# Strassen's partial sums kept in PSUM banks, adj and transition turned through DRAM and VectorE, layer norms applied on ScalarE, fewer weight loads and a longer lag, in a two-layer graph network kernel

## The chip, the cores and the metric

One core of one Trainium2 chip. The metric is the device time of one launch in microseconds (us), the median of several runs. A ratio of two kernels is the mean time of one kernel's fast runs over that of the other's fast runs of the same rounds on the same chip, so it is not quite the ratio of the medians quoted beside it.

## The reference

128 graphs of 128 nodes with 512 features; everything is fp32. Cut to what matters:

```python
# layer 0
deg = sum(adj, -1);  agg = (adj @ x) / max(deg, 1e-6)
y   = layernorm(x + relu(concat([x, agg]) @ W.T))
# layer 1: attention scores make a transition matrix, then K = 3 diffusion steps
e   = leaky_relu(sj[:, None] + si[:, None].T + ab)       # sj, si: y @ Wv @ aw
T   = adj * exp(e);  T = T / (sum(T, -1) + 1e-12)
H   = y @ Wk[0] + bk[0]  +  (T @ y) @ Wk[1] + bk[1]  +  (T @ T @ y) @ Wk[2] + bk[2]
out = layernorm(y + relu(H))
```

Both layers have the form "a product with weights, then a product with a 128x128 matrix of the graph".

## The kernel before

Two graphs make a pair, four a group; 64 pairs in all. The pair's products with weights are done in Strassen's way, with seven products of half the depth instead of eight, on sums of blocks. A product is two wide fp32 matmuls. The seven have to be combined: in the kernel before, ScalarE copies snapshots of a growing PSUM sum to SBUF, and VectorE adds them off to the side:

```python
def fused_pair(name, lf, rf, mT):              # used for layer 0 ("h") and the diffusion ("v")
    X, Y, W, V = ...                           # four PSUM banks; s: four SBUF snapshots
    product(X, 1, lf, rf, True);   nc.scalar.copy(s[0], X)
    product(Y, 2, lf, rf, True);   nc.vector.tensor_add(u[:, 0], Y, s[0])
    product(W, 5, lf, rf, True);   nc.scalar.copy(s[1], W)
    product(X, 6, lf, rf, False);  nc.scalar.copy(s[2], X)
    product(V, 4, lf, rf, True)
    product(X, 7, lf, rf, False);  nc.scalar.copy(s[3], X)
    nc.vector.tensor_add(u[:, 1], V, s[3])
    product(W, 3, lf, rf, False)
    nc.tensor.matmul(W, mT[0], u[:, 0], start=False, ...)   # product with adj or transition
    nc.tensor.matmul(X, mT[1], u[:, 1], start=False, ...)
    return (W, s[2]), (X, s[1])                # the caller adds the last snapshot

def layernorm(t):                              # VectorE, GpSimd, VectorE
    nc.vector.bn_stats(st, t);  nc.vector.bn_aggr(mv, st)
    nc.gpsimd.tensor_scalar(ve, mv[:, 1:2], LN_EPS, None, ALU.add)
    nc.gpsimd.tensor_tensor(rstd, ve, nhalf, ALU.pow)
    nc.vector.tensor_scalar(t, t, mv[:, 0:1], rstd, ALU.subtract, ALU.mult)
```

One step of the main loop runs layer 0 of a pair and layer 1 of the pair two steps earlier, so TensorE has two independent streams. The order of each engine's own instructions is set by a scheduler at build time. The traces show it kept: a sum whose inputs are there waits behind what was queued before it (the prediction below shows an add that ran 4.4 us late in this way). After layer 0's product, each of the two graphs gets its layer norm and two score sums (`scr`, VectorE, with a running sum as by-product).

Of the kernel before, what the change touches and what calls it, by code (L numbers as in the profile page):

```python
# [15 lines left out]
def kernel(  # L16
# [29 lines left out]

    nc = tc.nc
    P = 128
# [10 lines left out]
    const = ctx.enter_context(tc.tile_pool(name="const", bufs=1))  # L59
    p2 = ctx.enter_context(tc.tile_pool(name="p2", bufs=2))  # L60
    p1 = ctx.enter_context(tc.tile_pool(name="p1", bufs=1))
    p3 = ctx.enter_context(tc.tile_pool(name="p3", bufs=3))
    p4 = ctx.enter_context(tc.tile_pool(name="p4", bufs=4))
    dram = ctx.enter_context(tc.tile_pool(name="dram", bufs=3, space=bass.MemoryType.DRAM))
    small = ctx.enter_context(tc.tile_pool(name="small", bufs=4))
    ps_t = ctx.enter_context(tc.tile_pool(name="ps_t", bufs=2, space=bass.MemoryType.PSUM))
    ps_m = ctx.enter_context(tc.tile_pool(name="ps_m", bufs=6, space=bass.MemoryType.PSUM))
# [6 lines left out]
    def load_blocks(dst, src):  # L74

        for q in range(Q):
            nc.sync.dma_start(dst[q * R : (q + 1) * R].rearrange("r b j f -> r (b j) f"),
                              src[:, :, q * P : (q + 1) * P].rearrange("b (j r) f -> r (b j) f", r=R))
# [14 lines left out]


    def load_weight(dst, src):

        for q in range(Q):
            nc.sync.dma_start(dst[q * R : (q + 1) * R],
                              src[q * P : (q + 1) * P, :].rearrange("(c s) o -> s c o", s=R))

    load_x_blocks(0, 0)
    load_adj(0, nc.scalar)
    w0_sb = const.tile([P, 2 * NC, F], FP)
    wk_sb = const.tile([P, K, NC, F], FP)
    wvt_sb = [p4.tile([P, H, F], FP, name=f"wvt{i}", tag="y") for i in range(2)]
# [4 lines left out]
    load_weight(w0_sb[:, NC:, :], w0t[F:, :])  # L110
    load_weight(w0_sb[:, :NC, :], w0t[:F, :])
    load_x_blocks(0, 1)
    load_x(0, 0)
# [3 lines left out]
    nc.scalar.dma_start(bk_sb, bk)  # L117
    for i in range(2):
        nc.scalar.dma_start(wvt_sb[i], wvt[i * FH : (i + 1) * FH, :].rearrange("(c p) f -> p c f", p=P))
    load_adj(1, nc.scalar)  # L120
    load_x_blocks(1, 0)
    for k in range(K - 1, -1, -1):
        load_weight(wk_sb[:, k], wk[k])
# [5 lines left out]
    onesk = const.tile([K, P], FP)  # L129
    nc.gpsimd.memset(onesk, 1.0)  # L130
# [11 lines left out]
    w2, w1 = w0_sb[:, NC:, :], w0_sb[:, :NC, :]  # L142
# [8 lines left out]
    def fold_constants():  # L151
        for t in range(2):
            pw = ps_m.tile([P, F], FP, name="pw", tag="mm")
            for c in range(NC):
                nc.tensor.matmul(pw, aw_sb[:, t, c : c + 1].to_broadcast([P, P]), wvt_sb[c // H][:, c % H, :],
                                 start=(c == 0), stop=(c == NC - 1))
            nc.scalar.copy(wrow[:, t, :], pw)
        pb = ps_m.tile([P, F], FP, name="pb", tag="mm")
        nc.tensor.matmul(pb, onesk, bk_sb, start=True, stop=True)  # L159
        nc.scalar.copy(bias, pb)  # L160
        pc = ps_m.tile([P, F], FP, name="pc", tag="mm")
        for t in range(2):
            for c in range(NC):
                nc.tensor.matmul(pc[:, :1], bv_sb[:, c : c + 1].to_broadcast([P, P]), aw_sb[:, t, c : c + 1],
                                 start=(t == 0 and c == 0), stop=(t == 1 and c == NC - 1))
        nc.vector.tensor_add(cc, pc[:, :1], ab_sb)


    def transposed(dst, src):

        p = ps_t.tile([P, 4, P], FP, name="pt", tag="tr")
        for c in range(4):
            nc.tensor.transpose(p[:, c, :], src[:, c, :], ident)  # L173
        nc.scalar.copy(dst, p)

    def left_factors(pool, name, src):

        t = pool.tile([P, 7, H, P], FP, name=name)
        a11, a12, a21, a22, s1, s2, s4 = (t[:, i] for i in range(7))
        for i in range(2):  # L180
            nc.vector.transpose(t[:, 2 * i : 2 * i + 2].rearrange("p a h (j r) -> p j (a h) r", r=R),  # L181
                                src[:, i].rearrange("p j (c s) -> p j c s", s=R))
        nc.vector.tensor_add(s1, a21, a22)
        nc.vector.tensor_sub(a21, a11, a21)
        nc.gpsimd.tensor_sub(s2, s1, a11)
        nc.gpsimd.tensor_sub(s4, a12, s2)
        return [None, a11, a12, s4, a22, s1, s2, a21]

    def product(dst, i, lf, rf, start, stop=True):
        for c in range(H):  # L190
            nc.tensor.matmul(dst, lf[i][:, c, :], rf[i][:, c, :], start=(start and c == 0),  # L191
                             stop=(stop and c == H - 1), skip_group_check=True)

    def fused_pair(name, lf, rf, mT):


        X, Y, W, V = (ps_m.tile([P, F], FP, name=f"{name}{n}", tag="mm") for n in "xywv")
        s = [pool.tile([P, F], FP, name=f"snap{j}") for j, pool in enumerate((p1, p2, p2, p1))]
        u = p2.tile([P, 2, F], FP, name="u")
        product(X, 1, lf, rf, True)  # L200
        nc.scalar.copy(s[0], X)
        product(Y, 2, lf, rf, True)
        nc.vector.tensor_add(u[:, 0], Y, s[0])
        product(W, 5, lf, rf, True)
        nc.scalar.copy(s[1], W)
        product(X, 6, lf, rf, False)
        nc.scalar.copy(s[2], X)
        product(V, 4, lf, rf, True)
        product(X, 7, lf, rf, False)
        nc.scalar.copy(s[3], X)  # L210
        nc.vector.tensor_add(u[:, 1], V, s[3])  # L211
        product(W, 3, lf, rf, False)
        nc.tensor.matmul(W, mT[0], u[:, 0], start=False, stop=True, skip_group_check=True)  # L213
        nc.tensor.matmul(X, mT[1], u[:, 1], start=False, stop=True, skip_group_check=True)  # L214
        return (W, s[2]), (X, s[1])

    def layernorm(t):
        st = small.tile([P, 6], FP, name="st")
        nc.vector.bn_stats(st, t)  # L219
        mv = small.tile([P, 2], FP, name="mv")  # L220
        nc.vector.bn_aggr(mv, st)  # L221
        ve = small.tile([P, 1], FP, name="ve")
        nc.gpsimd.tensor_scalar(ve, mv[:, 1:2], LN_EPS, None, ALU.add)  # L223
        rstd = small.tile([P, 1], FP, name="rstd")
        nc.gpsimd.tensor_tensor(rstd, ve, nhalf, ALU.pow)  # L225
        nc.vector.tensor_scalar(t, t, mv[:, 0:1], rstd, ALU.subtract, ALU.mult)  # L226

    xfs, aTs, ys, ybs, yfs, scs, Ts, TTs = {}, {}, {}, {}, {}, {}, {}, {}
# [4 lines left out]
    def degree_norm(g):  # L233
# [6 lines left out]
        nc.vector.tensor_mul(an, adjs[g], rdeg[:, :, None].to_broadcast([P, G, N]))  # L240
        aTs[g] = p2.tile([P, G, N], FP, name="aT")
        transposed(aTs[g], an)

    def layer0(g, p):

        ys[g, p] = p4.tile([P, 2, F], FP, name="y")
# [5 lines left out]
        for i, (ph, s) in enumerate(hs):  # L252
            b = 2 * p + i
            y = ys[g, p][:, i, :]
            nc.vector.tensor_add(y, ph, s)
            nc.vector.scalar_tensor_tensor(y, y, 0.0, xs[g, p][:, i, :], ALU.max, ALU.add)
# [15 lines left out]
    def transition(g):  # L272
# [7 lines left out]
        T = p2.tile([P, G, N], FP, name="T")  # L280
# [10 lines left out]
        Ts[g] = T  # L291

    def t_transpose(g):
        TTs[g] = p2.tile([P, G, N], FP, name="TT")
        transposed(TTs[g], Ts[g])

    def layer1(g, p):
# [3 lines left out]
        v1 = p2.tile([P, 2, F], FP, name="v1", tag="u")  # L301
        for i, (pv, s) in enumerate(fused_pair("v", lf, f1, tT)):
            nc.vector.tensor_add(v1[:, i], pv, s)

        Q0, Q1 = (ps_m.tile([P, F], FP, name=f"o{i}", tag="mm") for i in range(2))
        Y, W, V, X = Q0[:, :FH], Q0[:, FH:], Q1[:, :FH], Q1[:, FH:]
        s = p1.tile([P, 2, F], FP, name="so")
        product(X, 1, lf, f2, True)
        nc.scalar.copy(s[:, 0, :FH], X)
        product(Y, 2, lf, f2, True)  # L310
        product(W, 5, lf, f2, False)
        nc.scalar.copy(s[:, 1, FH:], W)
        product(X, 6, lf, f2, False)
        nc.scalar.copy(s[:, 0, FH:], X)  # L314
        product(W, 3, lf, f2, False)
        product(X, 7, lf, f2, False)
        nc.scalar.copy(s[:, 1, :FH], X)  # L317
        nc.tensor.matmul(Q0, tT[0], v1[:, 0], start=False, stop=True, skip_group_check=True)  # L318
        product(V, 4, lf, f2, False)
        nc.tensor.matmul(Q1, tT[1], v1[:, 1], start=False, stop=True, skip_group_check=True)  # L320
        for i, q in enumerate((Q0, Q1)):
            nc.gpsimd.tensor_add(s[:, i], s[:, i], bias)  # L322
            nc.vector.tensor_add(s[:, i], q, s[:, i])  # L323
            r = ys[g, p][:, i, :]
            nc.vector.scalar_tensor_tensor(r, s[:, i], 0.0, r, ALU.max, ALU.add)  # L325
# [9 lines left out]
    f1 = weight_sums(nc.gpsimd, "t1", wk2[:, :H], wk1[:, :H], wk2[:, H:], wk1[:, H:])  # L335
    f2 = weight_sums(nc.gpsimd, "t2", wk0[:, :H, :FH], wk0[:, :H, FH:], wk0[:, H:, :FH], wk0[:, H:, FH:])
    steps = [(g, p) for g in range(NG) for p in range(2)]
    for t in range(len(steps) + 2):
# [7 lines left out]
        if t < len(steps):  # L346
            layer0(g, p)
            y_blocks(g, p)
        if g > 0 and p == 0:
# [5 lines left out]
        if t >= 2:  # L355
            layer1(*steps[t - 2])
        if t < len(steps):
            y_factors(g, p)
            if p == 1:
                transition(g)  # L360
# [25 lines left out]
```

## Time and profile before

| | before |
|---|---|
| time | 2366.9 us median of 4 runs (2364.1 to 2369.0) |
| TensorE busy | 2316.7 us of a span of 2367.8 |
| VectorE, ScalarE, GpSimd busy | 1607.1, 456.0, 627.7 us |
| granted TensorE clock | 0.993 |

The prediction below shows the page and the chain. Two stretches by window add the shape: the columns are the stretch, its length, the busy time of TensorE, its weight loads, VectorE, ScalarE, GpSimd with instruction counts, then the granted clock, the DMA engines' share and GB/s.

```profile
60.00:120.00 60.00, 40.51 (x106) 20.07 (x105) 33.36 (x71) 7.82 (x14) 12.65 (x18) 0.83 0.27 68
600.00:1000.00 400.00, 400.00 (x1137) 209.49 (x1136) 278.14 (x531) 78.26 (x150) 106.10 (x154) 1.00 0.27 77
```

TensorE is full from 180 to 2200 us. Behind the first loads, the hole of size is 19.5 us between 60 and 120 us.

Two groups of instructions will be wanted again (line, engine, operation, output and inputs, shape, count, then busy us and mean ns of one, then idle time before them):

```profile
L191 PE MATMUL vx<-t,yf 128*128 128x512 f32 x512 | 240.6, 592 | 0.0
L181 DVE STREAM_TRANSPOSE yf<-yb 128x512 f32<-128x512 f32 x128 | 83.6, 690 | 61.7 <-DMA yb<-yd 61.7
```

### The profile page before, as it was taken

The page shows a single profiled execution, that of the slowest core. Times are in us where ns is not written, and L with a number is a line of the kernel's source. Part 1 is how long each engine was busy: PE and PEld are TensorE (multiplying, and loading weights), DVE is VectorE, ACT ScalarE, POOL GpSimd, SP SyncE. Part 2 cuts the span into 40 slices and gives each one's busy share as a digit, 9 for nine tenths or more (in the row PEclk, how much of TensorE's full clock was granted, in tenths as well). Part 3 has the DMA queues.
Part 4 walks back from the last instruction along what each step waited for, and adds up shares of the span by engine and source line. Part 5 has one row for each costly group of instructions (what it writes and reads, how often), then busy time and mean ns, then how long its engine had stood idle before and what let it go on. Part 6 is the DMA issues. An engine that isn't in the chain of part 4 may idle for free.

```text
span 2367.8 us, 20175 instructions
## 1 busy us (share of the span) xinstructions
PE 2316.7 (98%) x6562; PEld 1213.0 (51%) x6562; DVE 1607.1 (68%) x3077; ACT 456.0 (19%) x868; POOL 627.7 (27%) x912
## 2 busy tenths in 40 slices
PE   6699999999999999999999999999999999999998
PEld 3355455455455455555555554554554554555554
DVE  5566667766767766767766677667677667676654
ACT  1111211211211211111111212112112112122111
POOL 3223222222222222322222232222222222222212
PEclk9899999999999999999999999999999999999999
DMA  9222322222223222223223223222222222232110
GB/s 209 69 83 71 93 62 81 85 67 80 76 76 85 67 83 82 67 81 89 67 72 94 67 76 91 63 79 84 67 85 75 76 80 67 85 85 63 45 54 27
DMA packets 212352, 183.81 MB, mean 78 GB/s; under 512 B 12563, under 2 KB 160019, under 8 KB 212246
## 3 DMA queue, kind: packets, MB, share of 16 engines
q1 hardware_dynamic: 210208, 180.93, 27.4%
q10 hardware_dynamic: 2038, 1.59, 0.3%
q8 instruction: 52, 0.85, 0.2%
q14 instruction: 54, 0.44, 0.1%
HBM read 115.36 MB, written 67.11 MB: 77 GB/s over the span
## 4 chain that ended last, share of the span: by engine, by line
PE 96%; DVE 2%; DMA 1%; POOL 0%; issue 0%; ACTq 0%; ACT 0%; POOLq 0%; DVEq 0%
PE o L191 16%; PE vx L191 14%; PE hx L191 14%; PE vw L191 9%; PE hw L191 9%; PE vv L191 5%; PE vy L191 5%; PE hv L191 5%; PE hy L191 4%; PE hx L214 2%; PE o L318 2%; PE vx L214 2%; PE vw L213 2%; PE hw L213 2%; PE o L320 2%; PE pt L173 1%
## 5 line engine op out<-in xcount | busy, mean ns | idle before, releaser
L322 POOL TENSOR_TENSOR so<-so,bias 128x512 f32<-128x512 f32 x128 | 168.0, 1313 | 683.9 <-ACT so L314 682.1
L223 POOL TENSOR_SCALAR ve<-mv 128x1 f32<-128x1 f32 x256 | 95.2, 372 | 949.2 <-DVE mv L221 944.5
L226 DVE TENSOR_SCALAR y<-y,mv,rstd 128x512 f32<-128x512 f32 x256 | 163.7, 640 | 169.6 <-POOL rstd L225 169.6
L191 PE MATMUL hw<-w_sb,xf 128*128 128x512 f32 x512 | 241.1, 593 | 3.2 <-DVE w_sb L137 3.2
L191 PE MATMUL hx<-t,xf 128*128 128x512 f32 x512 | 241.9, 595 | 0.0
L191 PE MATMUL o<-wk_sb,yf 128*128 128x256 f32 x1024 | 241.9, 379 | 0.0
L191 PE MATMUL vx<-t,yf 128*128 128x512 f32 x512 | 240.6, 592 | 0.0
L191 PE MATMUL vw<-wk_sb,yf 128*128 128x512 f32 x512 | 240.6, 592 | 0.0
L191 PEld LDWEIGHTS o<-wk_sb,yf 128*128 128x128 f32 x1024 | 194.6, 190 | 53.8 <-issue 30.1
L191 PE MATMUL o<-t,yf 128*128 128x256 f32 x768 | 197.1, 379 | 0.0
L260 DVE SCALAR_TENSOR_TENSOR scr<-y,wrow 128x512 f32<-128x512 f32 x256 | 182.6, 713 | 1.7 <-PE pb L159 0.3
L323 DVE TENSOR_TENSOR so<-o,so 128x512 f32<-128x512 f32 x128 | 87.6, 684 | 140.7 <-PE o L318 132.6
L219 DVE BATCH_NORM_STATS2 st<-y 128x6 f32<-128x512 f32 x256 | 170.7, 686 | 2.1
L191 PEld LDWEIGHTS o<-t,yf 128*128 128x128 f32 x768 | 145.7, 190 | 47.4 <-ACT so L317 27.6
L225 POOL TENSOR_TENSOR rstd<-ve,nhalf 128x1 f32<-128x1 f32 x256 | 162.5, 635 | 21.3
L191 PEld LDWEIGHTS hw<-w_sb,xf 128*128 128x128 f32 x512 | 97.2, 190 | 126.0 <-issue 121.7
L191 PEld LDWEIGHTS hx<-t,xf 128*128 128x128 f32 x512 | 97.7, 191 | 123.4 <-issue 122.6
L191 PEld LDWEIGHTS vw<-wk_sb,yf 128*128 128x128 f32 x512 | 97.3, 190 | 122.5 <-issue 122.5
L191 PEld LDWEIGHTS vx<-t,yf 128*128 128x128 f32 x512 | 97.3, 190 | 122.5 <-issue 110.5
L211 DVE TENSOR_TENSOR u<-hv,snap 128x512 f32<-128x512 f32 x64 | 44.2, 691 | 159.7 <-ACT snap L210 159.6
L325 DVE SCALAR_TENSOR_TENSOR y<-so,y 128x512 f32<-128x512 f32 x128 | 135.0, 1055 | 2.1
L181 DVE STREAM_TRANSPOSE yf<-yb 128x512 f32<-128x512 f32 x128 | 83.6, 690 | 61.7 <-DMA yb<-yd 61.7
(102 smaller groups left out, 3209.7 us busy)
## 6 DMA issues: line engine op xcount, KB each, us to landing
xb<-in_x_dram SPq DMA_DIRECT2D x256, 128.0 KB, 2.9
xg<-in_x_dram SPq DMA_DIRECT2D x64, 512.0 KB, 5.0
yd<-y SPq DMA_DIRECT2D x64, 512.0 KB, 3.1
yb<-yd SPq DMA_DIRECT2D x256, 128.0 KB, 3.2
out_dram<-y SPq DMA_DIRECT2D x64, 512.0 KB, 2.8
ag<-in_adj_dram SPq DMA_DIRECT2D x30, 256.0 KB, 2.7
wk_sb<-in_wk_dram SPq DMA_DIRECT2D x12, 256.0 KB, 8.6
w_sb<-in_w0t_dram SPq DMA_DIRECT2D x8, 256.0 KB, 8.4
```

The lines of the kernel that those rows point to most:

```text
L181: nc.vector.transpose(t[:, 2 * i : 2 * i + 2].rearrange("p a h (j r) -> p j (a h) r", r=R), src[:, i].rearrange("p j (c s) -> p j c s", s=R))
L191: nc.tensor.matmul(dst, lf[i][:, c, :], rf[i][:, c, :], start=(start and c == 0), stop=(stop and c == H - 1), skip_group_check=True)
L213: nc.tensor.matmul(W, mT[0], u[:, 0], start=False, stop=True, skip_group_check=True)
L214: nc.tensor.matmul(X, mT[1], u[:, 1], start=False, stop=True, skip_group_check=True)
L219: nc.vector.bn_stats(st, t)
L223: nc.gpsimd.tensor_scalar(ve, mv[:, 1:2], LN_EPS, None, ALU.add)
L225: nc.gpsimd.tensor_tensor(rstd, ve, nhalf, ALU.pow)
L226: nc.vector.tensor_scalar(t, t, mv[:, 0:1], rstd, ALU.subtract, ALU.mult)
L260: nc.vector.scalar_tensor_tensor(scr, y, 1.0, wrow[:, t, :], ALU.mult, ALU.mult, accum_out=scs[g][:, t, b : b + 1])
L322: nc.gpsimd.tensor_add(s[:, i], s[:, i], bias)
L323: nc.vector.tensor_add(s[:, i], q, s[:, i])
L325: nc.vector.scalar_tensor_tensor(r, s[:, i], 0.0, r, ALU.max, ALU.add)
```

## The change

Its intent: take VectorE's adds and the snapshots away by copying a partial sum once into a second PSUM bank, where TensorE then adds on; take the 64 groups of transposes from TensorE; fewer and larger weight loads (a matrix in two halves, not four quarters); apply the layer norms on ScalarE in place of VectorE; and fill the hole at the start by letting layer 1 lag three pairs. The core of the diff, cuts marked with "...":

```diff
     def fused_pair(name, lf, rf, mT):
-        X, Y, W, V = (ps_m.tile([P, F], FP, name=f"{name}{n}", tag="mm") for n in "xywv")
-        ...                                     (the form shown above)
+        X, Y, W, Z = (bank(f"{name}{n}") for n in "xywz")
+        product(X, 1, lf, rf, True)
+        nc.scalar.copy(Y, X)                    # PSUM to PSUM
+        product(Z, 5, lf, rf, True)
+        nc.scalar.copy(s5, Z)
+        product(X, 6, lf, rf, False)
+        nc.vector.tensor_add(W, X, s5)          # reads X: product 7 into X must wait for it
+        product(Y, 2, lf, rf, False)
+        nc.scalar.copy(u[:, 0], Y)
+        product(X, 7, lf, rf, False)
+        nc.vector.tensor_add(Z, X, s5)
+        product(W, 3, lf, rf, False)
+        product(X, 4, lf, rf, False)
+        nc.scalar.copy(u[:, 1], X)
+        nc.tensor.matmul(W, mT[0], u[:, 0], start=False, stop=True, skip_group_check=True)
+        nc.tensor.matmul(Z, mT[1], u[:, 1], start=False, stop=True, skip_group_check=True)
+        return W, Z
     def layernorm(t):
         ...
-        nc.vector.tensor_scalar(t, t, mv[:, 0:1], rstd, ALU.subtract, ALU.mult)
+        nc.gpsimd.tensor_scalar(shift, mv[:, 0:1], rstd, -1.0, ALU.mult, ALU.mult)
+        nc.scalar.activation(t, t, AF.Identity, bias=shift, scale=rstd)
     def left_factors(pool, name, src):
         ...
-                                src[:, i].rearrange("p j (c s) -> p j c s", s=R))
+                                src[:, i].rearrange("p j (s c) -> p j c s", s=R))
     def layer0(g, p):
-        transposed(aTs[g], an)                  # four TensorE transposes, a ScalarE copy
+        ans[g] = swap_blocks("an", an)          # to DRAM and back in blocks, then one
+        ...                                     # VectorE transpose; the same for T
     def load_weight(...):
-        for q in range(Q): ...                  # four quarter loads
+        eng.dma_start(dst[:, h * H : (h + 1) * H], src.rearrange("(p c) o -> p c o", c=NC)[...])
     def layer1(g, p): ...                       # output part likewise onto banks
-    for t in range(len(steps) + 2):
+    for t in range(len(steps) + 3):
         ...
-        if t >= 2: layer1(*steps[t - 2])
+        if t >= 3: layer1(*steps[t - 3])
```

Not shown: early matmuls into seven banks ("first"), a cheaper folding of constants, one more y buffer.

The names in the profile: h is layer 0, v the diffusion part, o the output part; hx is bank X of layer 0, vw bank W of the diffusion. "Product 7 of v" is a group `vx<-t,yf`.

## The prediction

> **What bounds the kernel now.** I read the page first (busy shares, slices, chain), then the chain in order of time for one pair, then the timeline of the engines around one pair, because the change puts other engines between TensorE's products.
>
> ```profile
> PE 2316.7 (98%) x6562; PEld 1213.0 (51%) x6562; DVE 1607.1 (68%) x3077; ACT 456.0 (19%) x868; POOL 627.7 (27%) x912
> ...
> PE   6699999999999999999999999999999999999998
> ...
> PE 96%; DVE 2%; DMA 1%; POOL 0%; issue 0%; ACTq 0%; ACT 0%; POOLq 0%; DVEq 0%
> ```
>
> TensorE is busy 98% and is 96% of the chain that ended last. The 51 us that it idles (2367.8 less 2316.7) lie nearly all in the first two slices and the end. In between it never waits, so only fewer TensorE instructions, a shorter fill or drain can make the kernel faster, and any new wait of TensorE makes it slower one for one. Cutting work on VectorE gives nothing by itself.
>
> The price list is in the chain, one pair of batches:
>
> ```profile
> 818.50 0.86 PE hw L213 x2
> 819.36 0.86 PE hx L214 x2
> 820.22 0.44 PE pt L173 x4
> 820.65 1.72 PE vx L191 x4
> ```
>
> A 512-wide matmul (two records) is 0.858 us, a product of two is 1.72, a group of four transposes 0.44. A pair is 16 wide matmuls for layer 0, 16 for the diffusion part, and 7.76 for the output part: 35.2 us. The chain shows 35.67 from one hx to the next (806.48 to 842.15), with one group of transposes in it.
>
> The handover times come from the timeline of the output part:
>
> ```profile
> 839.41 1.02 PE L318 MATMUL o<-v,TT 128*128 128x512 f32 x2
> ...
> 839.61 0.37 ACT L317 COPY so<-o 128x256 f32<-128x256 f32 x1 [1.35 <-PE o L191]
> 840.03 0.86 PEld L191 LDWEIGHTS o<-t,yf 128*128 128x128 f32 x4 [0.43 <-ACT so L317]
> 840.26 1.03 PE L191 MATMUL o<-t,yf 128*128 128x256 f32 x4
> ```
>
> ScalarE starts 0.20 us after the next matmul starts [...]. Its end reaches the next weight load 0.05 later, and the matmul 0.2 after that. With a 0.37 us copy this comes to 0.85, just inside the 0.86 of the one matmul between. So a wide copy with one wide matmul of cover will not fit.
>
> The last view is VectorE's and GpSimd's queue after a layer 0 product, where each layer norm waits for GpSimd:
>
> ```profile
> 895.10 0.16 DVE L221 BATCH_NORM_AGGREGATE mv<-st 128x2 f32<-128x6 f32 x1
> ...
> 896.34 0.94 DVE L226 TENSOR_SCALAR y<-y,mv,rstd 128x512 f32<-128x512 f32 x1 [0.77 <-POOL rstd L225]
> ...
> 899.20 0.55 DVE L226 TENSOR_SCALAR y<-y,mv,rstd 128x512 f32<-128x512 f32 x1 [0.45 <-POOL rstd L225]
> 899.66 0.68 DVE L260 SCALAR_TENSOR_TENSOR scr<-y,wrow 128x512 f32<-128x512 f32 x1
> 900.27 0.08 DVE L260 DVE_READ_ACCUMULATOR scr<-y,wrow 128x1 f32 x1
> 900.27 0.69 DVE L203 TENSOR_TENSOR u<-vy,snap 128x512 f32<-128x512 f32 x1
> ```
>
> The reader should see the last line: the vy product had ended at 895.70 (the next product's start in the timeline), yet its add ran at 900.27, 4.4 us late, behind two layer norms in VectorE's queue. Before, that lateness is free: the sum is needed only some 8 us later.
>
> [...] the 256-wide add xf L184 means 820 ns, while yf L183, the same shape, means 483. [...] the new block transfers move 128 B pieces, and the trace has the DMA engines 27% busy in mid-kernel, so I expect no bound there.
>
> **The change part by part.**
> 1. The transposes of adj and transition leave TensorE: 64 groups at 0.44, 28 us less on the path. VectorE takes 64 transposes at 0.69 instead, and the data goes through DRAM and back; a whole step is left for that.
> 2. Constants: 9.8 us of TensorE in the chain (6.87 + 1.05 + 1.88) become four wide matmuls, 3.4, with the rest inside the load time. About 6 us less.
> 3. Layer 1 lags three pairs. Before, TensorE idled 19.5 us between 60 and 120 us (40.5 busy of 60), waiting for the first transition; a third layer 0 pair now covers it. About 20 us less.
> 4. Loads. The seven first matmuls lie in the load time. But the first product now stands on TensorE behind a constant whose VectorE chain comes after the four weight sums (1.22 each), so it starts near 25 us, while before 3.4 us of products were done by 27.4. About 2 us worse. The tail loses an add but gains a GpSimd and ScalarE hop: 1 us less.
> Sum without new waits: 2366 - 28 - 6 - 20 + 2 - 1 = 2313.
> 5. VectorE per pair: out go 2 u adds of each fused product, 2 y adds, 2 v1 adds, 2 output adds (10 at about 0.69) and 4 normalisations (0.64), 9.4 us. In come four wide adds (0.69), three of 256 (0.42) and one transpose (0.69), 4.7. From 25.1 to about 20.4 us of 35. ScalarE rises from 7.1 to about 9.4, GpSimd loses 2.6 and gains four small shifts. None is a bound. But this gains nothing.
> 6. New waits on TensorE. In the built order, product 7 accumulates into the bank that W = X + s5 is read from, with only product 2 (1.72 us) between, so VectorE's add is now between two products: 0.20 + 0.69 + 0.05 + 0.2 = 1.14, slack 0.58. Product 4 and u1: the wide copy (0.586) has one matmul of cover: 0.20 + 0.59 + 0.05 + 0.2 = 1.03 against 0.86, a wait of 0.17, twice a pair: 64 x 0.34 = 22 us.
>
> The worst place is the diffusion add vw. It stands on VectorE behind all four score sums of layer 0 (L281), the last two of which wait for the second layer norm, now GpSimd (ve, rstd, shift) then ScalarE. With zero at the start of layer 0's first adjacency matmul: two transposes from 0.2, y at 1.43 and 2.11, the two statistics 2.72 and 3.32, aggregate 3.92. From there, as before, 1.2 to rstd; plus 0.35 shift, then 0.7 on ScalarE. On every second pair GpSimd does ve, rstd, shift twice in a row: second norm done near 7.6, score sums c and d (0.735 apart) to 9.2, add to 9.9, TensorE at 10.1. On the others its two xf subtractions (0.75 each) are queued between: second norm 9.3, add to 11.5, TensorE 11.7. TensorE itself would want product 7 at 1.91 + 1.72 + 0.43 + 3 x 1.72 = 9.2. Waits of 0.9 and 2.5, mean 1.7, in 61 pairs: 104 us. The add of layer 0 (hw) comes out just in time without the transition work in front of it, and 0 to 0.3 late with it: about 5 us.
> Sum of the waits: 22 + 104 + 5 = 131. 2313 + 131 = 2444. The large term rests on small differences of long queues; I shade it to about 85 and predict 2425 us.
>
> **The rivals.**
> - The waits are hidden. For it: VectorE, ScalarE and GpSimd all have less than 60% of work, and the order was made by a scheduler. If only the copy of u1 waits, 2313 + 22 = 2335; with none 2313, 2.2% faster. Against it: the vy add 4.4 us late in the trace of before shows that the real queue runs behind the order's assumption, and the new order has a longer chain at that place.
> - The waits add up further: stalls also at hw, at output product 7 (0.20 + 0.42 + 0.25 = 0.87 of 0.86) [...]. Another 0.5 to 1 us a pair makes 2470 to 2510.
> - Transfers become the bound: 128 B pieces and one queue with more waits make the transposed blocks late. Against it: 27% DMA share and three microseconds a landing, with 15 us or more to spare. If it came, single idle stretches of several us per group of four would cost up to 100 us.
>
> **Range and chances.** 2330 is almost all waits hidden, 2500 the second rival: 2330 to 2500. Faster by over 2% is below 2318.5, which needs every wait gone: 0.12. Within 2% (to 2413) needs the vw wait below about 1.2 us in the mean: 0.30. Slower: 0.58.
>
> **What would show it.** TensorE busy near 2275 to 2280 us with an idle of 130 to 160, no more bubble between 60 and 120 us. In the waits, TensorE's weight load vx waiting for VectorE's vw add for 50 us or more, and vz and hz of the adjacency matmul for ScalarE's u with about 0.2 each, 128 times. VectorE near 1310 us busy, ScalarE near 600. I am wrong if TensorE in mid-kernel is again busy in full (then time 2310 to 2335), if the vx wait is there but names ScalarE's s5 copy or the score sums come after the add, or if the transposed blocks from DRAM appear as releasers.

2313 us without new waits, plus 22 + 104 + 5 = 131 of waits, came to 2444, shaded to 2425. The rival's 0.5 to 1 us a pair is the author's guess. So are the 0.35 us for GpSimd's shift and the 0.7 for the norm on ScalarE, near what like instructions take in the trace of before: 0.37 for ve, and on ScalarE 0.59 for a copy (L207) and 0.63 for an ACTIVATE (L283) of 128x512.

## The result, and the profile after

The changed kernel takes 2584.1 us, median of 4 runs (2582.4 to 2584.3); the ratio to the kernel before is 1.0917 (95%: 1.0898 to 1.0936). It is slower, and by more than the range of the prediction allowed: 2584 against 2425, with 2500 as the upper end.

The page of the changed kernel, its busy line, then TensorE's waits (waiter, what it waited for: us in total, times, longest; PEld is the weight load of a matmul; in the prediction's timeline one starts at 840.03 us, its matmul at 840.26):

```profile
PE 2388.7 (93%) x6312; PEld 1188.0 (46%) x6312; DVE 1365.4 (53%) x2697; ACT 619.1 (24%) x1059; POOL 551.5 (21%) x1048
```

```profile
PE vx L201 <- DVE vw L214: 149.8, 57, 3.9
PE pb L165 <- DMA bk_sb<-in_bk_dram: 18.6, 1, 18.6
PE hx L201 <- DVE hw L214: 8.5, 29, 1.6
```

```profile
PEld vx L201 <- DVE vw L214: 198.4, 60, 4.7
...
PEld vz L223 <- ACT u L221: 42.8, 64, 2.2
```

The wait that was predicted is there, named as predicted: product 7 of the diffusion waits for VectorE's add vw. But TensorE is also busier than before, 2388.7 us with 250 records fewer. The groups say why:

```profile
L201 PE MATMUL vx<-t,yf 128*128 128x512 f32 x768 | 405.5, 654 | 151.1 <-DVE vw L214 149.8
L237 ACT ACTIVATE y<-y,shift,rstd 128x512 f32<-128x512 f32 x256 | 208.2, 813 | 837.1 <-POOL shift L236 837.0
...
L201 PE MATMUL vw<-wk_sb,yf 128*128 128x512 f32 x256 | 149.9, 716 | 0.0
...
L191 DVE STREAM_TRANSPOSE yf<-yb 128x512 f32<-128x512 f32 x128 | 138.7, 1086 | 0.0
```

The products behind the wait are slow: vw, which waits for nothing, takes 716 ns a record where 592 is normal. And a transpose of VectorE, 690 ns before, takes 1086. The windows that answer to those of before:

```profile
60.00:120.00 60.00, 53.24 (x134) 23.68 (x134) 45.14 (x93) 15.83 (x26) 15.77 (x28) 1.00 0.48 113
...
600.00:1000.00 400.00, 373.66 (x986) 186.06 (x985) 213.33 (x424) 96.33 (x165) 83.45 (x160) 0.97 0.31 83
```

The hole at the start has shrunk from 19.5 to 6.8 us, as meant. In mid-kernel, TensorE now idles 26 us in 400, at a granted clock of 0.97.

How the add comes so late is best seen in the timelines of one pair (start us, duration, engine, line; in brackets the idle time before it and who ended it). First VectorE:

```profile
1054.49 0.18 DVE L230 BATCH_NORM_AGGREGATE mv<-st 128x2 f32<-128x6 f32 x1
...
1056.99 0.69 DVE L281 SCALAR_TENSOR_TENSOR scr<-y,wrow 128x512 f32<-128x512 f32 x1 [1.02 <-ACT y L237]
...
1060.24 0.69 DVE L281 SCALAR_TENSOR_TENSOR scr<-y,wrow 128x512 f32<-128x512 f32 x1 [1.81 <-ACT y L237]
1060.86 0.08 DVE L281 DVE_READ_ACCUMULATOR scr<-y,wrow 128x1 f32 x1
1060.97 0.69 DVE L281 SCALAR_TENSOR_TENSOR scr<-y,wrow 128x512 f32<-128x512 f32 x1
1061.59 0.08 DVE L281 DVE_READ_ACCUMULATOR scr<-y,wrow 128x1 f32 x1
1061.59 0.69 DVE L214 TENSOR_TENSOR vw<-vx,s 128x512 f32<-128x512 f32 x1
```

ScalarE in the same stretch, then TensorE:

```profile
1056.14 0.81 ACT L237 ACTIVATE y<-y,shift,rstd 128x512 f32<-128x512 f32 x1 [1.93 <-POOL shift L236]
1059.39 0.81 ACT L237 ACTIVATE y<-y,shift,rstd 128x512 f32<-128x512 f32 x1 [2.44 <-POOL shift L236]
1060.11 0.56 ACT L212 COPY s<-vz 128x512 f32<-128x512 f32 x1
```

```profile
1057.31 1.88 PE L201 MATMUL vy<-wk_sb,yf 128*128 128x512 f32 x4
1062.34 1.98 PE L201 MATMUL vx<-t,yf 128*128 128x512 f32 x4 [3.15 <-DVE vw L214]
```

The sums that vw adds were there when vy began, at 1057.31. VectorE, at that moment, was in the score sums of another stage, and idled 1.81 us for ScalarE's second norm before it could go on in its order. ScalarE's copy s, the other operand of vw, stood behind the same norm. TensorE would have begun product 7 at about 1057.31 + 1.72 = 1059.03; it began at 1062.34, 3.3 us late. On the pair before, the same reading gives 1021.83 against 1019.49, 2.3 us late:

```profile
1021.83 2.45 PE L201 MATMUL vx<-t,yf 128*128 128x512 f32 x4 [2.19 <-DVE vw L214]
1024.08 3.15 PE L201 MATMUL vw<-wk_sb,yf 128*128 128x512 f32 x4
```

The slow matmuls stand here, behind the shorter of the two waits: four records in 2.45 and 3.15 us. By windows, the clock granted was 0.50 from 1024 to 1026 us, and 1.00 from 1062 to 1070, behind the longer wait.

### The profile page after: what moved, and what is told of

The parts are those of the page before. It is cut to its first block, busy times and chain, and to the rows that moved or that the text cites. A ratio compares the mean times of both kernels' runs of the same rounds, so it can differ in the third digit from the quotient of the medians.

```text
span 2582.3 us, 20595 instructions
## 1 busy us (share of the span) xinstructions
PE 2388.7 (93%) x6312; PEld 1188.0 (46%) x6312; DVE 1365.4 (53%) x2697; ACT 619.1 (24%) x1059; POOL 551.5 (21%) x1048
## 4 chain that ended last, share of the span: by engine, by line
PE 36%; issue 31%; DVE 16%; POOL 13%; ACT 2%; DMA 1%; SPq 0%; DVEq 0%; POOLq 0%; ACTq 0%
PE vx L201 10%; PE o L201 9%; PE vw L201 5%; PE hx L201 5%; POOL rstd L234 5%; DVE yf L191 3%; DVE y L347 3%; PE vz L223 2%; POOL shift L236 2%; DVE scr L281 2%; PE vw L222 2%; ACT y L237 2%; POOL ve L232 2%; POOL yf L196 2%; DVE st L228 2%
## 5 line engine op out<-in xcount | busy, mean ns | idle before, releaser
L201 PE MATMUL vx<-t,yf 128*128 128x512 f32 x768 | 405.5, 654 | 151.1 <-DVE vw L214 149.8
L237 ACT ACTIVATE y<-y,shift,rstd 128x512 f32<-128x512 f32 x256 | 208.2, 813 | 837.1 <-POOL shift L236 837.0
L201 PE MATMUL hx<-t,xf 128*128 128x512 f32 x768 | 364.4, 596 | 9.1 <-DVE hw L214 8.5
L201 PEld LDWEIGHTS vx<-t,yf 128*128 128x128 f32 x768 | 146.3, 197 | 364.7 <-DVE vw L214 198.4
L191 DVE STREAM_TRANSPOSE xf<-xb 128x512 f32<-128x512 f32 x128 | 136.5, 1090 | 167.2 <-PE hx L201 155.7
L201 PE MATMUL vw<-wk_sb,yf 128*128 128x512 f32 x256 | 149.9, 716 | 0.0
L191 DVE STREAM_TRANSPOSE yf<-yb 128x512 f32<-128x512 f32 x128 | 138.7, 1086 | 0.0
L201 PE MATMUL hx<-w_sb,xf 128*128 128x512 f32 x256 | 130.2, 593 | 0.0
L347 DVE SCALAR_TENSOR_TENSOR y<-o,y 128x512 f32<-128x512 f32 x128 | 86.3, 674 | 70.8 <-PE o L342 70.8
L201 PE MATMUL vx<-wk_sb,yf 128*128 128x512 f32 x256 | 120.8, 592 | 0.0
```

The costliest lines, as they stand in the source:

```text
L191: nc.vector.transpose(t[:, 2 * i : 2 * i + 2].rearrange("p a h (j r) -> p j (a h) r", r=R), src[:, i].rearrange("p j (s c) -> p j c s", s=R))
L201: nc.tensor.matmul(dst, lf[i][:, c, :], rf[i][:, c, :], start=(start and c == 0), stop=(c == H - 1), skip_group_check=True)
L237: nc.scalar.activation(t, t, AF.Identity, bias=shift, scale=rstd)
L347: nc.vector.scalar_tensor_tensor(r, q, 0.0, r, ALU.max, ALU.add)
```

## The experiments

Fourteen kernels ran; all gave the correct result. They are told in the order of the argument. The theory after the result, called A: nothing is too slow; the order on VectorE and ScalarE puts instructions of layer 0's tail (norms and score sums, with their hops between engines) in front of sums that TensorE waits for. Rivals: the new form of the product is slow in itself (C); the slower transposes are the cause (E); the hop of the norm to ScalarE is (F); the clock falls for another reason than the waits (D, P); the other parts of the change make the queue too long for any form of the product (G).

### r1 and r2: the same work, queued later

r1 queues the four score sums of layer 0 behind the diffusion's second add. r2 also queues the two norms behind ScalarE's copy s5. No instruction is added or taken away.

```diff
 def layer0(g, p): ...
-            layernorm(y)
-            for t in range(2): ... scr ...          # score sums
+            norms.append(layernorm(y))              # r2: the activation is emitted later
 ...
         if t >= 3: layer1(*steps[t - 3])
+        if t < len(steps):
+            with behind(("v", "5")):                # r2: ScalarE, after the copy s5 of "v"
+                while norms: norms.pop(0)()
+            y_blocks(g, p)
+            with behind(("v", "z")):                # r1, r2: VectorE, after Z = X + s5 of "v"
+                scores(g, p)
```

> Scores later: the four score sums of layer 0 are queued on VectorE behind the diffusion product's second add, everything else as changed. Theory A (queue order: the add vw waits behind layer 0's norms and score sums on VectorE, its operand s5 behind the second norm on ScalarE): the VectorE part of the wait goes, the ScalarE part stays; product vx waits 1.1 us on one pair and 2.5 on the other, mean 1.8 in place of 2.8, some of the slow clock recovers: about 2480 us (2450 to 2520). Theory B (only VectorE's order matters): no wait left, 2350. Theory C (adding onto banks written by other engines is itself slow, order without weight): unchanged, 2584.

r1: 2426.3 us (2424.3 to 2429.2), ratio 1.0245 (1.0230 to 1.0260). The order on VectorE alone was worth 158 us, more than I expected: 2426 lies outside the ranges of all three theories. Product 7 still waits, since s5 is late:

```profile
PE vx L201 <- DVE vw L214: 60.5, 57, 2.5
```

> Scores and norms later: as before, and layer 0's two norm activations are queued on ScalarE behind the copy s5 of the diffusion product. Theory A: the wait of product vx is gone (TensorE waits under 10 us for vw), the granted clock is back at 0.99, 2584 less 171 of waits less about 65 of slow clock: 2350 us (2330 to 2380). Theory C: unchanged near 2584. Theory D [...]: waits gone but the clock stays at 0.97 and the time near 2410.

r2: 2348.5 us (2348.3 to 2348.8), ratio 0.9916 (0.9901 to 0.9931). Its busy line, the groups that were slow, and the window:

```profile
PE 2305.1 (98%) x6312; PEld 1169.6 (50%) x6312; DVE 1349.4 (58%) x2697; ACT 619.9 (26%) x1059; POOL 504.4 (21%) x1048
```

```profile
L201 PE MATMUL vx<-t,yf 128*128 128x512 f32 x768 | 360.9, 592 | 0.0
L201 PE MATMUL vw<-wk_sb,yf 128*128 128x512 f32 x256 | 120.3, 592 | 0.0
```

```profile
600.00:1000.00 400.00, 398.68 (x1094) 202.64 (x1093) 237.67 (x476) 107.44 (x184) 82.96 (x177) 1.00 0.34 92
```

The wait is gone, and so is the slow clock. C falls: the bank sums are not slow (592 ns on banks that other engines wrote). Between the changed kernel and r2 lies the whole miss of the main term, 235.8 us by the two spans, and it can be split without a model, because both have the same 6312 records: idle time fell from 193.6 (2582.3 less 2388.7) to 41.4 us (2346.5 less 2305.1), 152 us; busy time fell from 2388.7 to 2305.1, 84 us. Most of the 84 is slower clock: 0.973 of 2582.3 us against 0.999 of 2346.5 is worth 67 us, an estimate from the two mean clocks. The other 17 were not followed up.

### r3 and r4: shorten the queue instead

r3 puts back the quarter weight loads, whose row order lets VectorE's transposes read contiguous rows. r4 applies the norms on VectorE again.

```diff
# r3
-        eng.dma_start(dst[:, h * H : (h + 1) * H], src.rearrange("(p c) o -> p c o", c=NC)[...])
+        for q in range(Q):
+            eng.dma_start(dst[q * R : (q + 1) * R, h * H : (h + 1) * H],
+                          src[q * P : (q + 1) * P].rearrange("(c s) o -> s c o", s=R)[...])
-                                src[:, i].rearrange("p j (s c) -> p j c s", s=R))
+                                src[:, i].rearrange("p j (c s) -> p j c s", s=R))
# r4
-        nc.gpsimd.tensor_scalar(shift, mv[:, 0:1], rstd, -1.0, ALU.mult, ALU.mult)
-        nc.scalar.activation(t, t, AF.Identity, bias=shift, scale=rstd)
+        nc.vector.tensor_scalar(t, t, mv[:, 0:1], rstd, ALU.subtract, ALU.mult)
```

> Quarter weights: the weight loads go back to four quarter loads with the old row order, so VectorE's transposes read contiguous rows again; all else as changed. Theory A: the transposes fall from 1.09 to 0.69 us, two of them stand before the late add in each pair, the vx wait shortens by 0.6 to 0.8 us: about 2535 us (2510 to 2555). Rival E (the layout is the main cause, queues then run on time): 2380. If the layout does not matter: 2584.

r3: 2496.4 us (2494.9 to 2497.0), ratio 1.0539. The transposes are back to 695 ns, the vx wait fell from 149.8 to 116.5 us and the clock rose to 0.985. That is 88 us where I expected 49: idle time fell by 41 us, and busy time by 46, of which the higher clock makes some 32 (an estimate from the two mean clocks: 0.027 of 2582.3 us less 0.015 of 2494.8). Still, most of the loss stays, so E is a part and not the cause.

> Norm on VectorE: the norms are applied by one VectorE instruction, as before the change, without GpSimd's shift and ScalarE's activation; score sums still in front of vw. Theory A: the chain in front of vw loses two hops and one shift, 0.5 to 1 us a pair, 2520 to 2550 us. Rival F (the hop to ScalarE is the main cause of the late add): 2400. If the wait is set elsewhere: 2584 or more, as VectorE gets 0.6 us of work four times a pair.

r4: 2650.9 us (2649.8 to 2652.2), ratio 1.1193: a clear miss, in the wrong direction. The waits show a second one beside the first:

```profile
PE vx L201 <- DVE vw L214: 125.4, 61, 2.7
PE hx L201 <- DVE hw L214: 112.0, 60, 2.5
```

The vx wait did get shorter, but now layer 0's own add hw is late on nearly every pair. The chain of r4 in order of time shows the reason (start, us, what):

```profile
1026.40 0.08 issue
1026.48 0.23 POOL ve L232
1026.71 0.07 issue
1026.79 0.58 POOL rstd L234
1027.42 0.43 issue
1027.85 0.70 DVE hw L214
1028.56 0.04 issue
1028.60 1.98 PE hx L201 x4
```

These are the norms of the output part of an earlier pair. With the norm on VectorE, VectorE waits for GpSimd's rstd up to four times a pair (0.41 to 0.78 us a wait in its timeline from 999 to 1042 us), and hw stands behind two of those. F falls, and A gets sharper: what matters is not only how long the queue is (r3), but that an engine which stops for a layer norm also serves TensorE.

### r5, r6 and r9: which engine does both

r5 is the changed kernel with the two fused products and their callers as before (snapshots by ScalarE, adds on VectorE); the rest of the change stays. r6 is the reverse: the kernel before with only the new fused products. r9 is r5 with the norm on VectorE, the edit of r4.

```diff
# r5, r9 (r6 the other way round)
-        ... fused_pair with bank sums ...; return W, Z
+        ... fused_pair with snapshots ...; return (W, s[2]), (X, s[1])
-            nc.vector.scalar_tensor_tensor(y, ph, 0.0, xs[g, p][:, i, :], ALU.max, ALU.add)
+            nc.vector.tensor_add(y, ph, s)
+            nc.vector.scalar_tensor_tensor(y, y, 0.0, xs[g, p][:, i, :], ALU.max, ALU.add)
```

> Snapshots back: the changed kernel with the two fused products (layer 0, diffusion) in their old form, sums taken by ScalarE's snapshots and added on VectorE off the path; transposes by DMA, whole weight loads, lag 3, norm on ScalarE and the new output part stay. Theory A (the bank sums put VectorE's late queue between two products): the vx and hx waits for VectorE are gone, since the late adds are needed only later; at most 0.4 us every second pair where a snapshot copy stands behind the second norm on ScalarE; TensorE near 99% in mid-kernel, 2330 us (2315 to 2350). Theory G (the longer queue itself, by whole loads, norms on ScalarE and the lag, holds TensorE whatever form the product has): over 2450.

r5: 2615.6 us (2609.2 to 2624.4), ratio 1.1056. The miss is mine: I had looked only at VectorE. ScalarE's timeline of r5:

```profile
1020.90 0.81 ACT L238 ACTIVATE y<-y,shift,rstd 128x512 f32<-128x512 f32 x1 [3.34 <-POOL shift L237]
1024.16 0.81 ACT L238 ACTIVATE y<-y,shift,rstd 128x512 f32<-128x512 f32 x1 [2.44 <-POOL shift L237]
1024.88 0.57 ACT L215 COPY snap<-vw 128x512 f32<-128x512 f32 x1
...
1025.65 0.58 ACT L217 COPY snap<-vx 128x512 f32<-128x512 f32 x1
```

The snapshot copies, which product 7 waits for, now stand behind ScalarE's norms; the wait list names them. The first half of this expectation (no wait for VectorE) was right, and the wait had moved to the other engine:

```profile
PE vx L201 <- ACT snap L217: 142.2, 59, 3.5
```

> Bank sums alone: the kernel before with only the two fused products in the new form [...]; transposes on TensorE, quarter weights, lag 2, norm on VectorE, old output part. Theory A: VectorE's queue with its waits for GpSimd's rstd now stands in front of the adds vw and hw, as in the run with the norm on VectorE: 2 to 4 us a pair, 2500 to 2640 us, the waits named vx for vw and hx for hw. Theory G: the old queue is fast enough, 2366 to 2400. The result may be numerically wrong[...].

r6: 2560.6 us (2559.9 to 2561.2), ratio 1.0817, with vx for vw at 107.2 us and hx for hw at 47.9. So the new products alone, in an otherwise old kernel with its norms on VectorE, cost 193 us.

> Snapshots back and norm on VectorE: the run with the old fused products (2615.6 us), and the norms applied on VectorE as before, so ScalarE has nothing but copies between products and VectorE nothing that a product waits for, save the three small adds of the output part. Theory A2 (any engine that both applies layer norms and stands between two products holds TensorE; the same sums on an engine free of norms do not): the snapshot waits of 281 us vanish, TensorE idle under 60 us, 2330 us (2310 to 2355). Theory G (the other parts of the change lengthen the queue and hold TensorE in any form): over 2450.

r9: 2322.9 us (2322.3 to 2323.6), ratio 0.9808 (0.9794 to 0.9823). TensorE's window:

```profile
600.00:1000.00 400.00, 400.00 (x1108) 207.48 (x1107) 298.49 (x573) 64.74 (x121) 76.36 (x136) 1.00 0.37 96
```

VectorE is busier than in the kernel before (1676.7 us, 72%), and TensorE does not wait in this window at all. G falls. Together the four kernels make a square, all with the changed loads, transposes and lag:

| | norm applied on ScalarE | norm applied on VectorE |
|---|---|---|
| bank sums: VectorE adds between products | 2584 (the change) | 2651 (r4) |
| snapshots: ScalarE copies between products | 2616 (r5) | 2323 (r9) |

Only one cell is fast: snapshots on an engine that applies no norms, and norms on an engine that stands between no two of the wide products. r2 reaches nearly the same (2348) with bank sums by order alone.

### r7 and r8: two smaller terms

r7 is r2 with the transposes of adj and transition back on TensorE. r8 is the kernel before with the lag of three alone.

```diff
# r7, on r2
-        ans[g] = swap_blocks("an", an)            # and the VectorE transpose; T likewise
+        ans[g] = an                               # later: transposed(aTs[g], ans.pop(g))
# r8, on before
-        if t >= 2: layer1(*steps[t - 2])
+        if t >= 3: layer1(*steps[t - 3])
```

> Transposes back on TensorE, on top of the run with scores and norms later (2348.5 us): adj and transition turned by TensorE and copied by ScalarE, no trip through DRAM. Step 1 of the prediction (64 groups at 0.44): 28 us more, 2376 us (2370 to 2385). Rival: the DMA and VectorE work beside them cost TensorE something too, then 2350 or less.

r7: 2384.5 us (2382.2 to 2386.7), 36.0 more than r2, where step 1 of the prediction had 28. The hw wait grew from 8.1 to 20.6 us, but TensorE's idle time in all did not (41.9 against 41.4): the 36 us are busy time, 37.6 more. Part of it is slower clock, at the start (0.91 in the first 120 us, 1.00 in r2): 0.994 of 2384.6 us against 0.999 of 2346.5 makes some 12 us, an estimate. The rest, some 26, is near the 28.

> Lag 3 alone: the kernel before with layer 1 lagging three pairs (and the factors of y one step later, one more y buffer). Step 3 of the prediction: the idle time of 19.5 us between 60 and 120 us shrinks to 0 to 7, 2350 us (2346 to 2356). Rival: the bubble is only moved, 2366.

r8: 2358.0 us (2355.4 to 2361.5), ratio 0.9963 (0.9948 to 0.9978): 9.6 us less than before, half of step 3's 20. TensorE was busy 51.70 of the 60 us between 60 and 120 us, in place of 40.51: the hole shrinks but does not close.

### r13 and r14: does the wait make the clock slow?

Twelve runs left one thing open: whether the slower matmuls come from the waits. r13 fills the wait with two spare wide matmuls into an unused bank; r14 has two spare matmuls of two columns in the same place, so it has the same order and an open wait. vw is pinned behind the score sums in both.

```diff
         product(Y, 2, lf, rf, False)
+        if name == "v":
+            spare = ps_t.tile([P, F], FP, name="spare", tag="tr")
+            ... 2 x nc.tensor.matmul(spare[:, :n], lf[2][:, 0, :], rf[2][:, 0, :n], ...)   # n = 512 or 2
         product(X, 7, lf, rf, False)
```

> Wait filled: the changed kernel with two spare 512-wide matmuls (1.7 us, into an unused bank) on TensorE between product 2 and product vx of the diffusion part, where it waits for vw; the late add is pinned behind the score sums as it was. Theory H (the clock falls because of idle waits of about 3 us): waits shrink below 2 us, the granted clock goes to 0.99 or more, vw's matmuls back from 716 to about 595 ns, and the time is 60 to 80 us below that of the run with open waits. Theory P (the clock falls for another reason): the clock stays near 0.97 and the time is that of the open run, since the wait was idle anyway.

> Wait open, the control: the same with spare matmuls of two columns. In both, the scheduler now puts hw behind the adjacency's scaling on every second pair, so both may lose up to 2 us there: 2590 to 2650 us. Theory H: clock near 0.97, vw near 716 ns. Theory P: as r13.

r13: 2773.2 us (2765.8 to 2782.8), clock 0.990. r14: 2827.3 us (2822.3 to 2827.7), clock 0.966. Both are far above what I wrote for r14 (2590 to 2650), because the scheduler answered the new instructions with another order in which layer 0's products wait too (hx for hw 71 us and for hy 67 us in both). The pair is still a fair one. The group of vw, in r13 and then in r14:

```profile
L201 PE MATMUL vw<-wk_sb,yf 128*128 128x512 f32 x256 | 125.7, 615 | 0.0
```

```profile
L201 PE MATMUL vw<-wk_sb,yf 128*128 128x512 f32 x256 | 153.4, 732 | 0.0
```

Filling the wait brought vw from 732 to 615 ns. TensorE's busy time without the spare matmuls fell from 2425.3 (2457.5 less 32.2) to 2357.1 us (2477.4 less 120.3): 68 us, although the same work was done and the idle time for vw was still 112 us in place of 191. The two mean clocks give the same 68 us (0.034 of 2825.4 less 0.010 of 2764.0). By the medians r13 is 54 us faster, a little under the 60 to 80 that H expected. H holds, P falls: TensorE had more work in r13 and a higher clock. The gaps make the following matmuls slow.

How long must a gap be? Over whole kernels the longer waits go with the lower clock: in the changed kernel the longest vx wait of the matmul was 3.9 us and of its weight load 4.7, at a clock of 0.973; in r1 they were 2.5 and 3.3, at 0.998. But r4 had a clock of 0.980, and by TensorE's own records no wait of it in mid-kernel was over 2.7 us. Wait by wait the length does not decide. The clock records of the changed kernel have 40 stretches at half clock. One lies at the very end; the other 39 are 3.41 us long each and began 0.1 to 1.4 us after a wait of product 7 for vw had ended. Such a stretch followed 15 of the 26 waits of 1.9 to 2.3 us and 24 of the 31 of 3.1 to 3.9 us, and none of the five waits of 1.2 to 1.6 us in the same kernel; 2.19 us of wait were followed by one and 3.15 us in the next pair were not (above). What decides was not tested.

### r10, r11 and r12: can it be made faster still?

r10 is r2 with the constants' matmuls behind product 4 of the first pair. r11 adds quarter weights. r12 is r9 with r10's edit, and the first turned adjacency ahead of the third pair's factors on VectorE.

```diff
# r10, r11, r12
-            fold_constants()
+            with tc.issue_after(early[4]): fold_constants()
# r12
-            x_factors(*steps[t + 2])
+            with tc.issue_after(turned[g]) if p == 0 else nullcontext(): x_factors(*steps[t + 2])
```

> Start freed: the run with scores and norms later (2348.5 us), and the constants' matmuls queued on TensorE behind product 4 of the first pair, so that the first product waits for weights alone and the early matmuls run while loading. First product at about 25 in place of 30.5 us, 5 us less: 2343 us (2338 to 2349).

r10: 2348.4 us, against 2348.5 of r2: nothing. The first product began at 17.07 in place of 30.35, but the first adjacency matmul at 46.70, as in r2 (46.71): its wait, in both timelines, ends with aT, the turned matrix on VectorE, whatever comes before.

> Start freed and quarter weights, on top of scores and norms later: transposes 0.69 in place of 1.09, so the hw waits of about 8 us go too; the quarter loads may land later by a few us. 2338 us (2330 to 2350). Within 2% of the kernel before in any case: TensorE's instructions alone sum to about 2300 us.

r11: 2338.3 us (2337.4 to 2340.5), ratio 0.9874 (0.9858 to 0.9891), as expected: the shorter transposes took the regular hw waits away.

> Best of both: the run with snapshots and the norm on VectorE (2323 us), the constants' matmuls behind product 4 of the first pair, and the first turned adjacency queued on VectorE ahead of the third pair's factors. There the first adjacency matmul stood 4.4 us behind the first pair's last product, and the first product stood behind constants: 4 us from the first, 0 to 4 from the second, 2317 us (2312 to 2322); against the kernel before 0.978 (0.976 to 0.981).

r12: 2322.6 us (2321.0 to 2323.6), ratio 0.9802 (0.9789 to 0.9816): the same as r9. The first pair's adjacency matmuls did end 9 us earlier, at 40.6 in place of 49.9, but a new wait takes it back at once:

```profile
PE hx L227 <- DVE u L224: 5.8, 1, 5.8
```

The next pair's add u stands on VectorE behind score sums, and the chain of r12 has those (58.20, L287) right after a load of the score row from DRAM that ends at 57.7. That row is made from the constants which the edit had moved back. r9 and r12 are the best versions: about 2% below the kernel before, where the interval of r9 lies across the mark of 2% and that of r12 too, so whether they are faster by 2% is unclear. Against the changed kernel r9 saves 261 us.

## Why the prediction was right or wrong

**What held.** The direction, the place and the name. Step 6 said that product 7 of the diffusion would wait for VectorE's vw, behind the score sums; that wait is the largest in the changed kernel, and moving exactly the score sums and norms (r1, r2) removes it. The sum without new waits, 2313, comes close to r9, in which no product waits in mid-kernel, at 2323; the lag and the constants, which brought 14 us less than expected (below), are enough for the difference. r9 has the old form of product, so this is a check of the sum and not of the change. VectorE near 1310 and ScalarE near 600 us were fair (1365 and 619), the third rival (transfers as the bound) did not come: none of TensorE's waits in mid-kernel names a DMA.

**What failed: the size of one term.** The prediction has "Waits of 0.9 and 2.5, mean 1.7, in 61 pairs: 104 us", shaded to 85. The runs put that term at 236 us (the changed kernel less r2). Two things were wrong in it: the waits were too short, and each was counted "one for one".

First, the waits themselves. Product 7 comes 2.3 and 3.3 us late on alternate pairs, not 0.9 and 2.5; in all, TensorE idles 152 us longer than in r2. The start was right, but links behind it were too short. The transposes were put at 0.69 from the trace of before; the new weight loads change the order of columns, so VectorE reads every fourth element, and two of them stand in front of the tail at 1.09 each (1086 ns in the mean; 695 with the old order of columns, in r3). Their own length is 2 x 0.40 x 61 pairs, 49 us; r3 undoes it and gets 88 us back. The norm on ScalarE was put at 0.7 and takes 0.81. On the pair that is 2.3 us late, the last two score sums took 0.86 and 1.09 us in place of 0.69, while GpSimd's subtractions of xf ran (1018.25 to 1020.61). And I let the copy s5 out: it stands behind the same norm on ScalarE. In the changed kernel it is not the last link (in the pair shown it ends at 1060.67, and vw begins at 1061.59), but shortening VectorE's queue alone (r1) leaves 60 us of wait. The prediction had listed the case "the vx wait is there but names ScalarE's s5 copy" as a sign of error; the wait names vw, and s5 stood hidden behind it.

Second, a term that was not in the sum at all: 84 us more of busy time, some 67 of it by a lower clock after those waits. The prediction said that "any new wait of TensorE makes it slower one for one"; the sum counted a wait as so much idle time and no more. r13 and r14 show that the gaps lower the clock: 0.966 with the wait open, 0.990 with it filled. The prediction's sign "TensorE busy near 2275 to 2280" (measured: 2388.7) failed mostly for this reason; with the waits gone it is 2305 in r2 and 2287 in r9.

**The shading.** The prediction cut 104 to 85 since "the large term rests on small differences of long queues". The runs show that such a difference is more apt to grow: the one link that was shortened by itself (r3) gave nearly twice its own length, because busy time fell with the wait (46 of the 88 us).

**The other terms.** The copy u1: 0.17 expected, 128 times, 22 us. The adjacency matmul behind it shows 0.94 in place of 0.86 in the chain of the changed kernel and of r2, 0.08 x 128, 10 us. hw: 5 expected, 8.5 measured. Transposes: 28 expected, 36 by r7, some 12 of it slower clock at the start. Lag: 20 expected, 9.6 by r8. Constants and loads together: 4 us better expected, but the second pair of r9 starts at 49.87 and that of the kernel before at 49.46, so nothing came of it; the turned adjacency is a new link in the start that the prediction had not looked at.

**The second rival** ("the waits add up further ... 2470 to 2510") was the nearest of the three, mostly for a reason it had not named: the same wait, larger, and a slow clock behind it. In the trace of the changed kernel, the 114 score sums that overlap a GpSimd subtraction took 0.83 us in the mean, the other 142 took 0.69. Its own stalls at hw and in the output part are small (8.5 and 0.6 us).

## What to carry to other kernels

Before moving an operand of the bounding engine from one engine to another, list what else that engine has to wait for: a helper that stops for someone else, as in a layer norm that hops over GpSimd, should not also stand between two products, however idle it looks by share (2616 and 2651 us here, against 2323). If it must, its order is the thing to set: here the same instructions take 2584 or 2348 us by order alone. And count a repeated wait of two to three us at more than its length where the clock granted falls with it: here 152 us of idle time brought some 67 us of slower matmuls.
